# Gated cross-attention and mixture of experts: the last routing step's rows at the far end of each expert's slots, and sixteen products ahead of them

## The chip, the cores and the metric

The kernel runs on one core of a Trainium2 chip. The metric is the device time of one execution in microseconds (us); the median of the runs counts. A profiled execution gives the trace from which single instructions are read.

## The reference

The computation is one decoder block on 4096 tokens of width D = 512. First comes a layernorm, a gated attention to 3202 context rows and a residual. Then comes a layernorm, a router that gives each token its two best of eight experts, the experts (512 to 2048 to 512, exact gelu), and a gated residual. Cut to the second part:

```python
gates = softmax(xf @ w_router + b_router)
topv, topi = top_k(gates, 2)
cap = int(1.25 * n / e)                      # 640 slots for each expert
pos = cumsum(one_hot(topi.reshape(-1)), axis=0)[...] - 1
keep = pos < cap                             # later rows are dropped
buf[e_flat, min(pos, cap - 1)] += where(keep, xf[tok], 0)
h = gelu(buf @ w1 + b1)
out = h @ w2 + b2
y = sum over k of w[:, k] * out[e, pos]      # w: gate, 0 if not kept
y = y / max(sum of w, 1e-6)
x = x + tanh(g_ffn) * y
```

The order of the tokens decides only who is kept when an expert has more than 640. Which of its slots a kept row takes doesn't matter to the result, as long as the row is brought back to its own token.

## The kernel before

The work that concerns the change is the end of the routing pass and the beginning of the experts.

**Routing pass.** The 4096 tokens are 32 tiles of 128. `STEPS` groups them: six steps of four tiles and then four steps of two. For a tile, `tile_mm` (line 1045) does eight accumulating matmuls into a bank pair `x1p` (line 1062), 264 columns each, which give the attention's output and the router's logits together. DVE adds the residual (`x1`, line 1066), ACT squares it for the variance (`jx`, line 1072) and stores the row. When a step's tiles are done, `scale` (line 1086) computes `rstd` on GpSimd (POOL, lines 1090 and 1091). `choose` (line 1093) takes the logits to one-hot choices on DVE, ending in `mask` (line 1149) and the running counts `base` (line 1157), while ACT writes the normalized rows `xn`. `place` (line 1159) lets PE count positions (`pos`, a matmul with a triangle of ones, `upper`, on `mask`, and one with `ones` on `base`, lines 1167 and 1168), and DVE turns them into slot indices `sidx` and weights. `dispatch` (line 1193) sends one tile's rows for one choice to their slots in the DRAM buffer `buf_d`: an indirect DMA issued by POOL, called a scatter here (line 1198). There are 64 scatters, two for each tile.

A step is software-pipelined over the next: `choose` of a step is written ahead of the tiles of the next one, `place` after the first two tiles of it (in a step of four tiles in the middle of the step, in one of two at its end), and `send` writes the scatters in groups of four or five around `scale`. `issue_after` pins an instruction's place in its engine's order to another one. On POOL a scatter that is written ahead of `rstd` runs ahead of it.

After the last tile PE has no tile left while the last step is chosen, placed and sent. `idle_work` fills that with matmuls whose result is not used: 7 of them ahead of the last `pos` and 11 behind it (line 1218).

**Experts.** Each expert's 640 slots are five blocks of 128. `expert_in` (line 1328) loads a block from `buf_d` (`xb`, issued by SP), transposes it on PE (`bps`, line 110) and copies it to `bT` (line 1344). For expert 0 each load waits for all 64 scatters. A product of two 2-by-2 blocked matrices is done with seven block products instead of eight (`seven`, line 1295); its block sums are taken on DVE (`T1` to `T4` of the rows, `w1s` of the weights). A product is `prod`: two accumulating matmuls, 320 columns in the first layer. The first layer has four such groups f for each half of the 2048 columns. In a group the order is `pa` (A11 B11, copied to `p1` by ACT), `p6`, `p7`, `pb`, then A12 B21 added to `pa`, whose gelu ACT writes to `h`, `p4`, and the rest of `pb`. DVE adds the parts (`u2`, `u3`, `h`). The products are named `pah`, `p6h` and so on in the profile (line 1299). After four groups comes the matmul chain `op` (line 1462) and the second layer.

Of the kernel before, what the change touches and what calls it, by code (L numbers as in the profile page):

```python
# [6 lines left out]
F32 = mybir.dt.float32  # L7
I32 = mybir.dt.int32
AF = mybir.ActivationFunctionType
# [5 lines left out]
P = 128  # L15
# [5 lines left out]
def gated_layer(ctx, tc, x, x_t, ctxt, ctxt_t, ctxt_c, ctxt_r, g_xattn, g_ffn, w_sim, w_sim_r, b_sim, W_qv, W_qv_t, b_qv, b_qv_c, w_router, b_router, w1, b1, w2, b2, out):  # L21
# [84 lines left out]
    def transposed(pool, src, name):  # L106

        ps = pool.tile([P, DC, P], F32, name=name, tag="tr")
        for c in range(DC):
            nc.tensor.transpose(ps[:, c, :], src[:, c * P : (c + 1) * P], ident)  # L110
        return ps

# [862 lines left out]
    with ExitStack() as s2:  # L975
# [49 lines left out]
        scatters = []  # L1025


        STEPS = [list(range(t, t + G)) for t in range(0, NT - 2 * G, G)]
        STEPS += [list(range(t, t + G // 2)) for t in range(NT - 2 * G, NT, G // 2)]
        qTs = {}  # L1030
        tt, ts, red = nc.vector.tensor_tensor, nc.vector.tensor_scalar, nc.vector.tensor_reduce
        stt = nc.vector.scalar_tensor_tensor
# [15 lines left out]
        def tile_mm(s, i):  # L1048
            t = s.tiles[i]
            g, q = divmod(t, 4)  # L1050
            if g not in qTs:
                qTs[g] = sb.tile([P, DC, TG], F32, name=f"q2T{g}", tag="q2T")
                ld = nc.sync.dma_start(qTs[g], qT_d[g])
                if g == 3:
                    with tc.issue_after(ld.ins):
                        load_half(0, 0)
            r = sb.tile([P, 2, BW], F32, name=f"r2_{t}", tag="r2", bufs=6)
            nc.sync.dma_start(r, r_d[t])
            ps = ps_mm.tile([P, 2, 512], F32, name=f"x1p{t}", tag="mm")
            for j in range(2):  # L1060
                for c in range(DC):
                    mm = nc.tensor.matmul(  # L1062
                        ps[:, j, :B1], qTs[g][:, c, q * P : (q + 1) * P], W1[:, c, j, :], start=(c == 0), stop=(c == DC - 1)
                    )
            x1 = sb.tile([P, D], F32, name=f"x1_{t}", tag="x1", bufs=G + 2)
            stt(
                x1.rearrange("p (j d) -> p j d", j=2), ps[:, :, :256], tgx, r[:, :, :256], ALU.mult, ALU.add,
                accum_out=s.sum[:, i : i + 1],
            )
# [23 lines left out]
        def choose(s):  # L1093
# [56 lines left out]
            for i in range(n):  # L1150
                if i + 1 < n:
                    dst = s.base[:, i + 1, :]
                elif s.next is not None:
                    dst = s.next.base[:, 0, :]
                else:
                    continue
                tt(dst, s.base[:, i, :], s.mask[:, i, :], ALU.add)

        def place(s):

# [33 lines left out]
            if s.next is not None and s.next.n == 2:  # L1194
                placed.append(done.ins)

        def dispatch(s, i, k):
            sc = nc.gpsimd.indirect_dma_start(
                out=buf_d[:, :],
                out_offset=bass.IndirectOffsetOnAxis(ap=s.sidx[:, k, i : i + 1], axis=0),  # L1200
                in_=s.xn[:, i, :],
                in_offset=None,
                bounds_check=E * CAP - 1,
                oob_is_err=False,
            )
            scatters.append(sc.ins)

            tc.declare_no_dep(scatters[-1], group="scatters", reason="slots are unique")
            tc.add_to_no_dep_group("scatters", scatters[-1])

        placed = []
        def idle_work(mm, n):

            for _ in range(n):
                with tc.issue_after(mm.ins):
                    mm = nc.tensor.matmul(idle, ones, wv[:, 0, :], start=True, stop=True)
            return mm

        idle = ps_id.tile([P, D], F32, name="idle", tag="idle")
        prev, s = None, begin(0)
        nc.vector.tensor_copy(s.base[:, 0, :], first_i)
        routed = []

        def send(n):
            for _ in range(min(n, len(routed))):
                dispatch(*routed.pop(0))

        def place_prev():  # L1230
            if prev is not None:
# [2 lines left out]

        for g in range(len(STEPS)):
            s.next = begin(g + 1) if g + 1 < len(STEPS) else None
            if prev is not None:
                choose(prev)
            for i in range(2):
                mm = tile_mm(s, i)  # L1240
            if s.n > 2:
                with tc.issue_after(mm.ins):
                    place_prev()
                send(4)
                for i in range(2, s.n):
                    tile_mm(s, i)
            sc = scale(s)
            if s.n == 2:
                with tc.issue_after(mm.ins):
                    place_prev()  # L1250
            with tc.issue_after(sc.ins):
# [14 lines left out]
    with ExitStack() as s3:  # L1266
# [25 lines left out]
            tt(S4, A12, S2, ALU.subtract)  # L1292
            return tt(A21, A11, A21, ALU.subtract)

        def seven(tag, n, A11, A12, A22, S1, S2, S3, S4, B11, B21, B22, T1, T2, T3, T4, done):

            def prod(ps, A, B, start=True, stop=True):
                for i, (a, b) in enumerate(zip(A, B)):
                    nc.tensor.matmul(  # L1299
                        ps, a, b, start=start and i == 0, stop=stop and i == len(A) - 1, skip_group_check=True  # L1300
                    )

            pa = bank(f"pa{tag}")[:, :n]
            prod(pa, A11, B11, stop=False)
            p1 = sb.tile([P, HC], F32, name=f"p1{tag}", tag="p1")[:, :n]
            nc.scalar.copy(p1, pa)  # L1306
# [11 lines left out]
            prod(pa, A12, B21, start=False)  # L1318
            done("11", pa, None)
            p4 = bank(f"p4{tag}")[:, :n]  # L1320
            prod(p4, A22, T4)
            done("21", p4, u3)
# [2 lines left out]

        row_loads, summed = [], {}

        def expert_in(e):
# [3 lines left out]
            xbs = []  # L1332
            for s in range(NST):
                xb = sb.tile([P, R], F32, name=f"xb{e}_{s}", tag="xb", bufs=NST)
                ld = nc.sync.dma_start(xb, buf_d[e * CAP + s * P : e * CAP + (s + 1) * P, :])
                row_loads.append(ld.ins)
                if e == 0:
                    for i in scatters:
                        tc.add_manual_dep(
                            ld.ins, i.name, mybir.DependencyInfo(mybir.DependencyClass.Sync, mybir.DependencyReason.DATA),  # L1340
                            reason="every token is in its slot",
                        )
                ps = transposed(ps_tr, xb, f"bps{e}_{s}")
                (nc.vector.tensor_copy if s % 2 else nc.scalar.copy)(xT[:, :, s * P : (s + 1) * P], ps)
# [39 lines left out]

        stored = []
        w1s = w1_sums(0, 0)
        nxt = expert_in(0)
        with tc.issue_after(row_loads[-1]):
            load_half(0, 1)
        for e in range(E):  # L1390
# [16 lines left out]
            for h in range(2):  # L1407
                W2 = weights.pop((e, h))[1] if (e, h) != (0, 0) else weights[0, 0][1]
                weights[e, h] = (None, W2)
                hT = cb.tile([P, KH, CAP], F32, name=f"h{e}_{h}", tag="h")  # L1410
                hS = [cb.tile([P, KQ, MH], F32, name=f"hs{k}_{e}_{h}", tag=f"hs{k}") for k in (1, 2, 4)]
                for f in range(KQ):
                    col = e * NF + h * KH + f
# [16 lines left out]
                    seven(f"h{e}_{h}_{f}", HC, *A, *xs, hidden)  # L1430

                    left_sums(
                        hS[0][:, f, :], hS[1][:, f, :], hS[2][:, f, :],
# [120 lines left out]
```

## Time and profile before

| | |
|---|---|
| three runs | 2636.52, 2637.51 and 2645.64 us |
| median | 2637.51 us |
| profiled execution, its own time | 2642.18 us |
| its span in the trace | 2640.2 us |
| mean granted TensorE clock | 0.995 |
| PE busy | 2609.3 us, 99% |
| DVE, ACT, POOL busy | 1703.0, 462.6 and 236.6 us |
| routing matmuls `x1p` | 512 records, 117.5 us |
| expert transposes of block 0 start | 1631.75 us |
| `p6h` of the first group starts | 1639.34 us |
| `op` of the first half starts | 1667.43 us |

Times within the trace count from the start of the span. Each matmul of 32-bit floats shows as two records or so, so counts of records are larger than those in the code. PE, PEld, DVE, ACT, POOL and SP are the matmul and the weight load of TensorE, VectorE, ScalarE, GpSimd and the queue engine SyncE. A row of the profile gives the line, engine, operation, output and inputs, the number, the busy time and mean duration of one, and then the idle time of the engine ahead of it with what ended most of it.

### The profile page before, as it was taken

What the parts mean: (1) busy time and instruction counts of PE and PEld (TensorE: products, weight loads), DVE (VectorE), ACT (ScalarE), POOL (GpSimd) and SP (SyncE); (2) the same over time, 40 slices, a digit from 0 to 9 for tenths busy, and PEclk for the clock granted to TensorE, in tenths of its full rate; (3) what the DMA queues carried; (4) which work ended last, traced back from release to release, by engine and by line L of the source; (5) the groups of instructions that cost most, each with busy time, mean ns of one, the idle gap of its engine ahead of it and who ended that gap; (6) DMA issues with size and microseconds to landing.
All of it is one profiled execution on the core that took longest, in us unless ns stands there. A gap on an engine that the chain in (4) does not pass through costs nothing. (4 is left out here: it accounts for less than half of the span.)

```text
span 2640.2 us, 29718 instructions
## 1 busy us (share of the span) xinstructions
PE 2609.3 (99%) x11236; PEld 2104.7 (80%) x11236; DVE 1703.0 (65%) x3412; ACT 462.6 (18%) x796; POOL 236.6 (9%) x288
## 2 busy tenths in 40 slices
PE   8999999999999999999999998999999999999998
PEld 7748888888888888888888885777777777777776
DVE  7868856947768569478475566474757565565654
ACT  1201201201102002012020143212121111111111
POOL 0111000000001000000000155010101010101010
PEclk9999999999999999999999999999999999999999
DMA  8496656746747657467445794231324132223210
GB/s 316 150 290 234 207 180 192 244 149 179 255 158 196 220 162 239 159 189 245 153 144 203 279 351 162 79 124 64 128 72 145 71 128 88 104 92 100 76 60 20
DMA packets 182959, 436.07 MB, mean 165 GB/s; under 512 B 17454, under 2 KB 84270, under 8 KB 180768
## 3 DMA queue, kind: packets, MB, share of 16 engines
q1 hardware_dynamic: 150208, 352.25, 40.4%
q0 software_dynamic: 16096, 45.04, 5.0%
q10 hardware_dynamic: 16512, 36.88, 4.0%
q8 instruction: 89, 1.46, 0.2%
q14 instruction: 54, 0.44, 0.1%
HBM read 355.71 MB, written 85.55 MB: 167 GB/s over the span
## 5 line engine op out<-in xcount | busy, mean ns | idle before, releaser
L512 PE MATMUL pas<-Qp,kt 128*128 128x256 f32 x672 | 160.5, 380 | 0.0
L1299 PE MATMUL pah<-bT,w 128*128 128x320 f32 x512 | 159.3, 433 | 0.5 <-ACT p1h L1306 0.5
L662 PE MATMUL pbv<-E,vt 128*128 128x256 f32 x672 | 147.3, 379 | 0.0
L662 PEld LDWEIGHTS pbv<-E,vt 128*128 128x128 f32 x672 | 127.7, 190 | 17.4
L512 PEld LDWEIGHTS pas<-Qp,kt 128*128 128x128 f32 x672 | 127.1, 190 | 17.4 <-ACT hqT L720 0.2
L1299 PEld LDWEIGHTS pah<-bT,w 128*128 128x128 f32 x512 | 97.0, 190 | 39.7 <-ACT p1h L1306 1.0
L602 DVE TENSOR_TENSOR E<-E,mb 128x1024 f32<-128x1024 f32 x96 | 116.2, 1226 | 11.8 <-ACT mb L589 11.8
L603 ACT ACTIVATE E<-E 128x1024 f32<-128x1024 f32 x96 | 101.0, 1058 | 129.5 <-DVE E L602 128.7
L1299 PE MATMUL pao<-w,h 128*128 128x256 f32 x512 | 120.9, 379 | 0.0
L1062 PE MATMUL x1p<-W,q2T 128*128 128x264 f32 x512 | 117.5, 391 | 0.0
L1485 POOL DMA_INDIRECT out<-acc,ti x40 | 41.1, 1027 | 851.6 <-DVE acc L1484 841.8
L1462 PE MATMUL op<-w,h 128*128 128x512 f32 x256 | 114.8, 592 | 0.0
L1299 PEld LDWEIGHTS pao<-w,h 128*128 128x128 f32 x512 | 97.3, 190 | 20.1 <-issue 7.7
L1062 PEld LDWEIGHTS x1p<-W,q2T 128*128 128x128 f32 x512 | 97.8, 192 | 16.5
L468 ACT COPY p1s<-pas 128x512 f32<-128x512 f32 x48 | 28.1, 586 | 439.1 <-issue 257.0
L538 DVE TENSOR_TENSOR M<-M,E 128x1024 f32<-128x1024 f32 x80 | 98.0, 1225 | 4.3
L693 PE MATMUL vv<-E,vc 128*128 128x512 f32 x192 | 95.2, 627 | 0.0
L1462 PEld LDWEIGHTS op<-w,h 128*128 128x128 f32 x256 | 46.6, 190 | 48.7 <-issue 43.0
L1423 DVE TENSOR_TENSOR h<-p4h,u3h 128x320 f32<-128x320 f32 x64 | 31.3, 490 | 78.0 <-PE p4h L1299 76.3
L481 ACT COPY E<-pas 128x512 f32<-128x512 f32 x48 | 28.1, 586 | 303.9 <-PE pas L512 287.6
L484 DVE TENSOR_TENSOR E<-p4s,u3s 128x512 f32<-128x512 f32 x48 | 33.1, 689 | 73.5 <-PE p4s L512 73.5
L611 DVE TENSOR_TENSOR SM<-SM,E 128x1024 f32<-128x1024 f32 x64 | 78.7, 1229 | 2.5 <-ACT E L603 2.5
(449 smaller groups left out, 5470.4 us busy)
## 6 DMA issues: line engine op xcount, KB each, us to landing
kt<-kt_d SPq DMA_DIRECT2D x84, 896.0 KB
w<-in_w SPq DMA_DIRECT2D x32, 2048.0 KB
vt<-vs_d SPq DMA_DIRECT2D x56, 768.0 KB
wp<-wt_d SPq DMA_DIRECT2D x56, 520.0 KB
kt_d<-ktb ACTq DMA_DIRECT2D x12, 896.0 KB
buf_d<-zero SPq DMA_DIRECT2D x80, 129.0 KB
xb<-buf_d SPq DMA_DIRECT2D x40, 258.0 KB
r<-r_d SPq DMA_DIRECT2D x32, 260.0 KB
```

The lines of the kernel that those rows point to most:

```text
L484: tt(done(1, 0), p4, u3, ALU.add)
L512: nc.tensor.matmul(ps[:, jl, :], kts[j][:, KSLOT[p], k, :], B[p][:, k, :], start=start and jl == 0 and k == 0, stop=stop and k == 1, skip_ ...
L538: tt(M, M, e[:, :, h], ALU.max)
L602: live[g]["last"] = tt(e, e, m, ALU.subtract)
L603: live[g]["exp"] = nc.scalar.activation(e, e, AF.Exp)
L611: tt(SM, E_t[0][:, lr] if jj == 1 else SM, E_t[jj][:, lr], ALU.add)
L662: nc.tensor.matmul(ps[b], vt[:, j - i * JH, b * P : (b + 1) * P], right(j) if j < NJ else right_c, start=start and j == 0 and b == 0, stop ...
L693: mm = nc.tensor.matmul(ps[b], vc[:, h, b * P : (b + 1) * P], E[j // 2][:, :, h, j % 2, :] if j < NJ else ec, start=j == 0 and h == 0, sto ...
L1062: mm = nc.tensor.matmul(ps[:, j, :B1], qTs[g][:, c, q * P : (q + 1) * P], W1[:, c, j, :], start=(c == 0), stop=(c == DC - 1))
L1299: nc.tensor.matmul(ps, a, b, start=start and i == 0, stop=stop and i == len(A) - 1, skip_group_check=True)
L1462: nc.tensor.matmul(ps, hT[:, k, 2 * MH :], W2[:, k, :], start=(k == 0), stop=(k == KH - 1))
L1485: sc = nc.gpsimd.indirect_dma_start(out=out[:, :], out_offset=rows_of(ti, s), in_=acc[:, :], in_offset=None, bounds_check=N - 1, oob_is_er ...
```

## The change

1. The last twelve tiles are stepped 3, 3, 2, 2, 2 where they were 4, 2, 2, 2, 2: the sizes are five steps of four and then these five.
2. The last step's rows take the slots from the far end of each expert (the last slot first) instead of those behind the earlier rows. For this one matmul (`first`) sums the counts, and four DVE operations turn the position round. The last step's four scatters are kept in a list of their own, `late`. Of expert 0's five blocks the first three wait for the 60 other scatters alone, the last two for all.
3. For expert 0, `early_products` does A11 B11 and A12 B21 of the four groups of the first half (16 matmuls, `pe`) as soon as the first three blocks are transposed. `seven` then leaves these two products out in those groups. The order on PE is block 0, 1, 2, products of f = 0, 1 and 2, blocks 3 and 4, products of f = 3.
4. `idle_work` does 7 and 5 matmuls where it did 7 and 11, with the identity, broadcast, as moving operand in place of `wv`.
5. Places in the engines' orders: the second tile's `x1` in steps of two follows `choose`'s count, scatters are chained one after the other, the groups of `send` are 4, 3 or 5 by the size of the step. Block 1's copy to `bT` is ACT's for expert 0.

```diff
-        STEPS = [list(range(t, t + G)) for t in range(0, NT - 2 * G, G)]
-        STEPS += [list(range(t, t + G // 2)) for t in range(NT - 2 * G, NT, G // 2)]
+        STEPS, sizes = [], [G] * (NT // G - 3) + [3, 3, 2, 2, 2]
...
+            with tc.issue_after(chosen[-1]) if s.n == 2 and i else ExitStack():
+                stt(x1..., accum_out=s.sum[:, i : i + 1])
...
+            if s.next is None:
+                before = T("before", [P, 2, n, E])
+                tt(before, s.first.unsqueeze(1).unsqueeze(1).to_broadcast([P, 2, n, E]), s.oh, ALU.mult)
+                s.far = T("far", [P, 2, n])
+                red(s.far, before, AX.X, ALU.add)
+                stt(s.far, s.rv, -float(CAP), s.far, ALU.mult, ALU.add)
...
+            if s.next is None:
+                stt(pos, s.far, float((E + 1) * CAP - 1), pos, ALU.add, ALU.subtract)
...
-            scatters.append(sc.ins)
+            (scatters if s.next is not None else late).append(sc.ins)
...
-                    mm = nc.tensor.matmul(idle, ones, wv[:, 0, :], start=True, stop=True)
+                    mm = nc.tensor.matmul(idle, ones, ident.unsqueeze(1).to_broadcast([P, 4, P]), start=True, stop=True)
...
-                send(4)
+                with tc.issue_after(scaled[-1].ins) if scaled else ExitStack():
+                    send(4)
...
+                s.first = ps_mm.tile([P, 2, 512], F32, name="first", tag="mm")[:, 0, :E]
+                    mm = nc.tensor.matmul(s.first, ones, s.base[:, 0, :], start=True, stop=True)
...
-                send(4 if s.n > 2 else 5)
+                send({4: 4, 3: 3, 2: 5}[s.n])
...
-        idle_work(prev.counted, 11)
+        idle_work(prev.counted, 5)
...
-                    for i in scatters:
+                    for i in scatters if (s + 1) * P <= CAP - len(late) // 2 * P else scatters + late:
...
+                if amid is not None and s * P < HC <= (s + 1) * P:
+                    between = amid(*([xT[:, k, :HC] for k in c] for c in ((0, 1), (2, 3))))
+                    behind = [next(between) for _ in range(KQ - 1)][-1]
...
+        def early_products(B11, B21):
+            early["h"] = hT = cb.tile([P, KH, CAP], F32, name="h0_0", tag="h")
+            mm = None
+            for f in range(KQ):
+                A11, A12 = ([a[:, k, f * P : (f + 1) * P] for k in range(2)] for a in w1s[:2])
+                pa = bank(f"pe{f}")[:, :HC]
+                with tc.issue_after(mm.ins) if mm is not None else ExitStack():
+                    prod(pa, A11, B11, stop=False)
+                early[f] = cb.tile([P, D], F32, name=f"e1_{f}", tag=f"o{f}")[:, :HC]
+                nc.scalar.copy(early[f], pa)
+                last = prod(pa, A12, B21, start=False)
+                nc.scalar.activation(hT[:, f, :HC], pa, AF.Gelu, bias=b1_t[:, f : f + 1])
+                mm = yield last
```

More of the change, by code (lines that the diff above doesn't have):

```diff
@@ L109, in transposed @@
         for c in range(DC):
-            nc.tensor.transpose(ps[:, c, :], src[:, c * P : (c + 1) * P], ident)
+            moved.append(nc.tensor.transpose(ps[:, c, :], src[:, c * P : (c + 1) * P], ident))
         return ps
+    moved = []
     NJ = L // (2 * P)
@@ L1023, in gated_layer @@
         nc.gpsimd.iota(first_i, pattern=[[NST, E]], base=0, channel_multiplier=0)
-        scatters = []
-        STEPS = [list(range(t, t + G)) for t in range(0, NT - 2 * G, G)]
-        STEPS += [list(range(t, t + G // 2)) for t in range(NT - 2 * G, NT, G // 2)]
+        scatters, late = [], []
+        STEPS, sizes = [], [G] * (NT // G - 3) + [3, 3, 2, 2, 2]
+        for n in sizes:
+            t = STEPS[-1][-1] + 1 if STEPS else 0
+            STEPS.append(list(range(t, t + n)))
+        assert STEPS[-1][-1] == NT - 1
         qTs = {}
@@ L1065, in tile_mm @@
             x1 = sb.tile([P, D], F32, name=f"x1_{t}", tag="x1", bufs=G + 2)
[L1066 to L1069, printed above, removed]
+            with tc.issue_after(chosen[-1]) if s.n == 2 and i else ExitStack():
+                stt(
+                    x1.rearrange("p (j d) -> p j d", j=2), ps[:, :, :256], tgx, r[:, :, :256], ALU.mult, ALU.add,
+                    accum_out=s.sum[:, i : i + 1],
+                )
             junk = sb.tile([P, D], F32, name=f"jx{t}", tag="jx", bufs=2)
@@ L1156, in choose @@
                     continue
-                tt(dst, s.base[:, i, :], s.mask[:, i, :], ALU.add)
+                chosen.append(tt(dst, s.base[:, i, :], s.mask[:, i, :], ALU.add).ins)
+            if s.next is None:
[4 more added lines that the diff above has]
+                stt(s.far, s.rv, -float(CAP), s.far, ALU.mult, ALU.add)
         def place(s):
@@ L1193, in place @@
             )
-            if s.next is not None and s.next.n == 2:
+            if s.next is not None and s.next.n < G:
                 placed.append(done.ins)
@@ L1205, in dispatch @@
             )
-            scatters.append(sc.ins)
-            tc.declare_no_dep(scatters[-1], group="scatters", reason="slots are unique")
-            tc.add_to_no_dep_group("scatters", scatters[-1])
-        placed = []
+            (scatters if s.next is not None else late).append(sc.ins)
+            tc.declare_no_dep(sc.ins, group="scatters", reason="slots are unique")
+            tc.add_to_no_dep_group("scatters", sc.ins)
+        placed, chosen = [], []
         def idle_work(mm, n):
@@ L1217, in idle_work @@
                 with tc.issue_after(mm.ins):
-                    mm = nc.tensor.matmul(idle, ones, wv[:, 0, :], start=True, stop=True)
+                    mm = nc.tensor.matmul(idle, ones, ident.unsqueeze(1).to_broadcast([P, 4, P]), start=True, stop=True)
             return mm
         idle = ps_id.tile([P, D], F32, name="idle", tag="idle")
-        prev, s = None, begin(0)
+        prev, s, scaled = None, begin(0), []
         nc.vector.tensor_copy(s.base[:, 0, :], first_i)
@@ L1227, in send @@
             for _ in range(min(n, len(routed))):
-                dispatch(*routed.pop(0))
+                with tc.issue_after((scatters[-1:] + late[-1:])[-1]) if scatters else ExitStack():
+                    dispatch(*routed.pop(0))
         def place_prev():
@@ L1247, in gated_layer @@
             sc = scale(s)
+            scaled.append(sc)
             if s.n == 2:
@@ L1250, in gated_layer @@
                     place_prev()
+                mm = prev.counted
+            if s.next is None:
+                s.first = ps_mm.tile([P, 2, 512], F32, name="first", tag="mm")[:, 0, :E]
+                with tc.issue_after(mm.ins):
+                    mm = nc.tensor.matmul(s.first, ones, s.base[:, 0, :], start=True, stop=True)
             with tc.issue_after(sc.ins):
-                send(4 if s.n > 2 else 5)
+                send({4: 4, 3: 3, 2: 5}[s.n])
             prev, s = s, s.next
@@ L1293, in left_sums, with prod, seven @@
             return tt(A21, A11, A21, ALU.subtract)
[L1295 to L1306, printed above, removed]
+        def prod(ps, A, B, start=True, stop=True):
+            for i, (a, b) in enumerate(zip(A, B)):
+                mm = nc.tensor.matmul(
+                    ps, a, b, start=start and i == 0, stop=stop and i == len(A) - 1, skip_group_check=True
+                )
+            return mm
+        def seven(tag, n, A11, A12, A22, S1, S2, S3, S4, B11, B21, B22, T1, T2, T3, T4, done, p1=None):
+            there = p1 is not None
+            if not there:
+                pa = bank(f"pa{tag}")[:, :n]
+                prod(pa, A11, B11, stop=False)
+                p1 = sb.tile([P, HC], F32, name=f"p1{tag}", tag="p1")[:, :n]
+                nc.scalar.copy(p1, pa)
             p6 = bank(f"p6{tag}")[:, :n]
@@ L1317, in seven @@
             done("22", pb, u3)
-            prod(pa, A12, B21, start=False)
-            done("11", pa, None)
+            if not there:
+                prod(pa, A12, B21, start=False)
+                done("11", pa, None)
             p4 = bank(f"p4{tag}")[:, :n]
@@ L1326, in gated_layer, with expert_in @@
         row_loads, summed = [], {}
-        def expert_in(e):
+        def expert_in(e, amid=None):
             xT = cb.tile([P, DC, CAP], F32, name=f"bT{e}", tag="bT")
@@ L1331, in expert_in @@
             ti = sb.tile([P, NST], I32, name=f"ti{e}", tag="ti", bufs=E)
-            xbs = []
+            xbs, behind = [], None
             for s in range(NST):
@@ L1342, in expert_in @@
                         )
-                ps = transposed(ps_tr, xb, f"bps{e}_{s}")
-                (nc.vector.tensor_copy if s % 2 else nc.scalar.copy)(xT[:, :, s * P : (s + 1) * P], ps)
-                xbs.append(xb)
+                with tc.issue_after(behind.ins) if behind is not None else ExitStack():
+                    ps = transposed(ps_tr, xb, f"bps{e}_{s}")
+                (nc.vector.tensor_copy if s % 2 and (amid is None or s > 2) else nc.scalar.copy)(
+                    xT[:, :, s * P : (s + 1) * P], ps
+                )
+                xbs.append(xb)
+                if amid is not None and s * P < HC <= (s + 1) * P:
+                    between = amid(*([xT[:, k, :HC] for k in c] for c in ((0, 1), (2, 3))))
+                    behind = [next(between) for _ in range(KQ - 1)][-1]
+            if amid is not None:
+                between.send(moved[-1])
             B11, B12, B21, B22 = (xT[:, r : r + 2, c : c + HC] for r in (0, 2) for c in (0, HC))
@@ L1386, in gated_layer @@
         w1s = w1_sums(0, 0)
-        nxt = expert_in(0)
+        early = {}
+        def early_products(B11, B21):
[5 more added lines that the diff above has]
+                with tc.issue_after(mm.ins) if mm is not None else ExitStack():
+                    prod(pa, A11, B11, stop=False)
+                early[f] = cb.tile([P, D], F32, name=f"e1_{f}", tag=f"o{f}")[:, :HC]
[3 more added lines that the diff above has]
+                mm = yield last
+        nxt = expert_in(0, early_products)
         with tc.issue_after(row_loads[-1]):
@@ L1409, in gated_layer @@
                 weights[e, h] = (None, W2)
-                hT = cb.tile([P, KH, CAP], F32, name=f"h{e}_{h}", tag="h")
+                hT = early.pop("h") if "h" in early else cb.tile([P, KH, CAP], F32, name=f"h{e}_{h}", tag="h")
                 hS = [cb.tile([P, KQ, MH], F32, name=f"hs{k}_{e}_{h}", tag=f"hs{k}") for k in (1, 2, 4)]
@@ L1429, in gated_layer @@
                     A = [[a[:, k, f * P : (f + 1) * P] for k in range(2)] for a in w1s]
-                    seven(f"h{e}_{h}_{f}", HC, *A, *xs, hidden)
+                    seven(f"h{e}_{h}_{f}", HC, *A, *xs, hidden, early.pop(f, None))
                     left_sums(
```

## The prediction

> **What bounds the kernel now.** I read the page first, its busy shares and its costliest groups.
>
> ```profile
> PE 2609.3 (99%) x11236; PEld 2104.7 (80%) x11236; DVE 1703.0 (65%) x3412; ACT 462.6 (18%) x796; POOL 236.6 (9%) x288
> ...
> L1299 PE MATMUL pah<-bT,w 128*128 128x320 f32 x512 | 159.3, 433 | 0.5 <-ACT p1h L1306 0.5
> ...
> L1062 PE MATMUL x1p<-W,q2T 128*128 128x264 f32 x512 | 117.5, 391 | 0.0
> ```
>
> TensorE (PE) is busy 99% of 2640.2 us, so the whole change plays for the time in which PE has nothing useful, at the passage from the routing pass to the experts. That passage is seen in the table of windows (after the length, each engine's busy time, PE first; third from the right PE's clock) and then in the timeline of PE:
>
> ```profile
> 1598.00:1600.00 2.00, 0.28 (x2) 0.00 (x0) 1.83 (x13) 1.21 (x4) 1.39 (x3) 1.00 0.40 144
> 1600.00:1602.00 2.00, 1.43 (x6) 1.36 (x7) 0.69 (x5) 0.00 (x0) 0.88 (x1) 0.70 0.10 22
> 1602.00:1604.00 2.00, 2.00 (x6) 1.49 (x6) 1.81 (x9) 0.81 (x2) 0.20 (x1) 0.50 0.10 38
> ...
> 1632.00:1634.00 2.00, 2.00 (x10) 1.73 (x10) 0.27 (x1) 0.59 (x1) 0.00 (x0) 0.50 0.99 314
> ```
>
> ```profile
> 1600.57 0.37 PE L1167 MATMUL pos<-mask,upper 128*128 128x16 f32 x2 [2.29 <-DVE eq L1131]
> ...
> 1610.26 6.25 PE L1218 MATMUL idle<-wv,ones 128*128 128x512 f32 x14
> 1617.90 0.37 PE L1167 MATMUL pos<-mask,upper 128*128 128x16 f32 x2 [1.39 <-DVE mask L1149]
> 1618.12 0.37 PE L1168 MATMUL pos<-base,ones 128*128 128x16 f32 x2
> 1618.34 9.69 PE L1218 MATMUL idle<-wv,ones 128*128 128x512 f32 x22
> 1631.75 3.59 PE L110 MATMUL bps<-ident,xb 128*128 128x128 f32 x16 [3.72 <-DMA xb<-buf_d]
> ```
>
> The last tile of x1p ends at 1610.1; the first transpose of expert rows (bps) starts at 1631.75. Between them stand filler (idle, two records for each matmul of 0.86 to 0.88 us), pos, and 1.39 and 3.72 us of nothing. What ends last there is the chain of scatter, DMA and load, in the timeline of POOL:
>
> ```profile
> 1619.28 0.98 POOL L1198 DMA_INDIRECT buf_d<-xn,sidx  x1 [0.30 <-issue]
> 1621.54 1.23 POOL L1198 DMA_INDIRECT buf_d<-xn,sidx  x1 [1.28 <-issue]
> ...
> 1626.61 0.98 POOL L1198 DMA_INDIRECT buf_d<-xn,sidx  x1 [0.30 <-issue]
> ```
>
> The last scatter ends at 1627.59, SP issues the row loads at 1628.99, bps starts 2.76 later. PE then needs until 1639.34 for p6h of f=0, from where it has no gap.
>
> **What the Trainium skill says.** "TensorE: Matmul & The Clock Gate", Part 1, has the clock halved after an idle window of about 3.4 us that runs freely. The trace agrees in kind: after the 2.29 and the 3.72 us gaps PE ran 3.41 us at 0.50, costing 1.7 us each; after 1.39 it did not. "DMA: Bandwidth & Descriptors", on one DMA's anatomy, gives about 2.0 us fixed; the 2.76 us from load issue to transpose fits. "ScalarE: Activation LUTs", on ACT_TABLE_LOAD, gives 1283 ns; the trace has 1.28 at 1639.41, before the first gelu.
>
> **The change part by part**, on the clock of the profiled execution. That took 2642.18 (span 2640.2 plus 1.98), 4.67 above the median 2637.51. I put this down to its gap at 1598.28 to 1600.57: DVE's x of tile 28 waited 1.80 us for a signal that came 2.8 us after that tile's last matmul, then came the half clock: 2.3 + 1.7 of the 4.67. So an ordinary execution has p6h at about 1639.34 - 4.67 = 1634.7.
>
> 1. *Early products.* 16 matmuls are 8 products; one is 2 x 538 = 1.076 us (320 columns, pace of the h stage: 26 products in the 28.1 us to 1667.43). Before, 2 of them stand ahead of p6h, so 6 x 1.076 = 6.46 us move from behind it to ahead of it. It is a gain only if PE has free time there.
>
> 2. *Late step apart.* Blocks 0 to 2 need only the first 60 scatters; scatter 60 ended at 1620.26 where the last ended at 1627.59. So up to 7.3 us come free, if scatter 60 doesn't move. Blocks 3 and 4 still wait for all 64; SP holds xb3, xb4 and the loads of the next half's weights behind that wait, none of them needed earlier than 3 us after pe starts.
>
> 3. *Step sizes.* Sizes 4,4,2,2,2,2 at the end become 4,3,3,2,2,2 (tiles 20-22, 23-25). In a step of over two tiles, pos of the step before stands after two tiles of the next: pos(5) now stands behind tile 24, not 25. Its mask needs rstd(5), which on POOL stands behind four scatters of step 4. They ran at 1571.74 to 1576.54, started by xn(4), and the change doesn't touch that. So rstd(5) ends at 1577.8 (1.3 us for the pair), mask 3.8 later (choose with a stt inside took 3.74 to 3.88) at 1581.6. PE is through tile 24 at 1578.5: **3.3 us idle**. pos(5) 1581.85, tile 25 from 1582.6. Next, place(5) (2.4, and 0.75 to the first scatter) puts three scatters at 1586.45 to 1590.05 ahead of rstd(6): mask(6) 1595.1, pos(6) 1595.35; tile 27 ended at 1593.2: **2.15 us idle**. A half clock after the first gap (1.7) is hidden in the second. Then tiles 28 to 31 run to 1610.9, with no wait at pos(7) (its 2 tiles are 7.1, the chain 5.9) and 0.6 at pos(8). An ordinary run of before, without the lateness, has x1p end at 1606.1. So these stalls give back 4.8 us.
>
> 4. *The tail after.* pos(8) 1611.5, xn 1614.9, four scatters 1615.65 to 1620.8 (0.97 + 0.30 each), loads 1.4 later, bps at **1624.9**. Filler is 12 instead of 18, ending at about 1623.0 (6 x 0.87 = 5.2 less): 1.9 us idle, between a gap that halved the clock and one that did not. pe starts after three blocks, 3.5 later, 1628.4. Six products take 6.46; ACT has behind them the table load (1.28), four copies of 0.43 and gelus of 0.53 which must release banks: I take 1.65 us of waits. 1636.5 less the overlaps: 1636.1. bps 3 and 4, 1.8; the last two products and a copy, 2.8: p6h at **1640.8**. The late scatters end near 1628, so their blocks are there by 1632 and don't bind.
>
> 5. *Small parts.* first: one matmul of 128x8, under 0.3 us on PE, in filler's place. before, far and two stt: four DVE operations of about 0.2 us; one (0.2) lies on the late scatters' path, which has 4 us of slack; the others beside filler. Chained dispatches: POOL issues in that order already, nothing; if the cover of POOL's spare time were gone it would be 0.3 each. The broadcast identity instead of wv in filler: same columns, bound -0.1 to +0.1 each, hidden by the gap. b_1's load ahead on SP: 64 KB, 0.3 us, behind the row loads.
>
> The copy of block 1 on ACT instead of DVE takes 0.59 for 0.69: nothing, since blocks arrive about 1 us apart. The second tile's stt after choose in steps of two tiles: at most 0.75 earlier mask, 0.75 later rstd; choose without a stt inside took 2.98. I take zero and keep both ends.
>
> Sum: p6h at 1640.8 with 6.46 less behind it counts as 1634.3, against 1639.34 in the profiled execution (-5.0) and 1634.7 in an ordinary run (-0.4). With half a chance of 1.7 for the 1.9 us gap it is +0.5; if the ACT waits vanish (bound 0 to 1.65) it is -1.2. An ordinary run at 2637.5 - 1.2 to + 0.5; I take the lower half, **2636.5**.
>
> **The rivals.**
>
> *A, about the same (0.52): 2634.5 to 2638.5*, as summed.
>
> *B, the tail's gain stays (0.30): 2630 to 2634.* For it: PE's gaps at pos(5) and pos(6) rest on POOL's pace, and the second exists only if scatters of step 5 are ready before rstd(6)'s input; were rstd(6) first, 2.15 us are back, and with the ACT waits gone 3.8: 2637.1 - 3.8 = 2633.3; without the first gap too, 2630. Or the lateness of tile 28 is regular in before and goes with the new order: again 2.3 to 4. Against it: POOL's order in the change has rstd(5) behind four scatters, and two of three runs lie 5 us below the profiled one.
>
> *C, slower (0.15): 2639.5 to 2644.* In the first f groups PE has 5 products each instead of 7: 20 x 1.076 = 21.5 us. DVE was busy 22.24 of the 28.09 us of that stretch, and its work doesn't shrink. If DVE sets the pace, PE waits from f=1 on for banks: 22.24 - 21.5 = 0.7, with the T sums of 0.8 each that now lie nearer 2 to 3; a throttle at both gaps that isn't hidden adds up to 3.4: 2637.1 + 2 to 6. It decides when DVE is more than 90% busy between p6h and op. Against: w2 sums (4 x 1.22) can be done during op's 4.7 us.
>
> *D, the change doesn't do what it says (0.03):* the wait on SP or bank reuse keeps pe behind the late scatters; then 2637 to 2641.
>
> **How the numbers follow.** A measurement of this kernel can tell about 0.5%, 13.2 us, from no change. No part reaches it: all that could be gained is the 6.46 moved plus 5 of tail, all that was priced as a loss 5 + 3.4. So within 0.5% has 0.94, faster 0.04 (several unknowns at once), slower 0.02 (before's own runs reach 2645.64). The forecast is A's, 2636.5. The range takes B from 2630 and C up to 2642.
>
> **What would show it.** In the profile after: PE idle 3 us ahead of pos after tile 24 and 2 us ahead of the next pos, released by DVE mask; bps 5 to 7 us earlier (1624 to 1626); the gap ahead of it about 2 us; six pe products with short waits on ACT before bps 3; p6h near 1641; h stage without PE gaps. Wrong if PE has no gap at those pos (then B), if p6h to op takes over 23 us (C), or if bps 0 starts after the last scatter's landing (D).

## The result, and the profile after

The changed kernel takes 2645.4 us (median of 7 runs, 2645.22 to 2647.45), against 2637.51 before (7 runs): a ratio of 1.003, 95% interval 1.002 to 1.0039. It is 7.9 us slower. The forecast was 2636.5 with a range up to 2642.0. So a small gain was forecast and a loss measured; the time is still within 0.5% of before's, as the forecast also said.

The page of the changed kernel has PE busy for the same share as before. PE's work is shorter by 5 us, about what six filler matmuls took, in a longer span:

```profile
span 2643.3 us, 29700 instructions
...
PE 2604.4 (99%) x11226; PEld 2102.5 (80%) x11226; DVE 1700.6 (64%) x3415; ACT 462.8 (18%) x797; POOL 227.5 (9%) x288
```

The timeline of PE shows where the time is (start, length, then what; in brackets the idle time ahead and what ended it):

```profile
1582.58 0.59 PE L1181 MATMUL pos<-mask,upper 128*128 128x24 f32 x2 [3.12 <-DVE mask L1156]
1583.00 0.60 PE L1182 MATMUL pos<-base,ones 128*128 128x24 f32 x2
1583.43 13.68 PE L1068 MATMUL x1p<-W,q2T 128*128 128x264 f32 x48
...
1619.98 4.54 PE L1235 MATMUL idle<-ident,ones 128*128 128x512 f32 x10
1633.67 3.02 PE L110 MATMUL bps<-ident,xb 128*128 128x128 f32 x12 [9.16 <-DMA xb<-buf_d]
1637.37 4.82 PE L1324 MATMUL pe<-bT,w 128*128 128x320 f32 x16 [0.68 <-ACT bT L1378]
1642.84 2.42 PE L1324 MATMUL pe<-bT,w 128*128 128x320 f32 x8 [0.65 <-ACT e L1440]
...
1648.90 1.24 PE L1324 MATMUL p6h<-x,w1s 128*128 128x320 f32 x4
```

The gap at pos(5) is there, 3.12 us long. But the first bps stands at 1633.67, where 1624.9 was forecast, behind a gap of 9.16 us. POOL and SP say why:

```profile
1620.92 0.98 POOL L1214 DMA_INDIRECT buf_d<-xn,sidx  x1 [0.30 <-issue]
1623.28 1.23 POOL L1214 DMA_INDIRECT buf_d<-xn,sidx  x1 [1.38 <-issue]
...
1628.36 0.98 POOL L1214 DMA_INDIRECT buf_d<-xn,sidx  x1 [0.30 <-issue]
```

```profile
1630.74 2.23 SPq L1367 DMA_DIRECT2D xb<-buf_d  x5
```

The first row is scatter 60, issued by 1621.90. The load of block 0 is not issued behind it but at 1630.74, 1.4 us after the end of scatter 64. All five loads go out together within 2.23 us, as they did before. So the last step's rows are not apart from the others: the loads still wait for them.

For comparing traces I count from pos of step 4. Up to about there all versions do the same work in the same order, and what they do differently comes behind it. Executions reach it at 1564.9 to 1568.9, and that of free at 1574.2, where PE stood still for 4.53 us ahead of pos(2) and had a half clock behind it. "Rest" runs from p6h to the end of the trace. The row of before is an execution of 2638.38 us, near its median; the trace shown ahead of the prediction is of a slower one. Its bps and p6h are these:

```profile
1628.34 3.71 PE L110 MATMUL bps<-ident,xb 128*128 128x128 f32 x16 [3.78 <-DMA xb<-buf_d]
...
1635.53 1.34 PE L1299 MATMUL p6h<-x,w1s 128*128 128x320 f32 x4
```

| us from pos(4) | last x1p ends | scatter 60 ends | scatter 64 ends | first load | first bps | p6h | rest |
|---|---|---|---|---|---|---|---|
| before (2638.38) | 39.67 | 50.52 | 57.64 | 59.04 | 61.87 | 69.06 | 1000.82 |
| after (2645.33) | 44.96 | 54.22 | 61.65 | 63.05 | 65.99 | 81.22 | 994.41 |
| free | 43.79 | 53.05 | 60.72 | 54.47 | 57.33 | 71.82 | 994.41 |
| oldsteps | 39.66 | 48.83 | 55.84 | 57.24 | 60.08 | 76.70 | 994.41 |
| free_oldsteps | 39.66 | 48.83 | 55.84 | 50.24 | 53.13 | 69.94 | 994.41 |
| steps_only | 49.11 | 57.94 | 65.20 | 66.60 | 69.42 | 77.10 | 1000.82 |
| late_alone | 39.68 | 48.86 | 55.89 | 50.27 | 53.28 | 65.78 | 1000.71 |
| fill7 | 39.65 | 48.81 | 55.82 | 50.22 | 53.23 | 67.49 | 994.41 |
| fill7_gelu | 39.65 | 48.84 | 55.84 | 50.24 | 53.13 | 67.51 | 994.41 |
| rstd_first | 42.76 | 51.61 | 59.00 | 53.02 | 55.83 | 73.32 | 994.41 |
| idle11 | 43.78 | 56.28 | 63.61 | 65.02 | 67.79 | 84.42 | 994.40 |

The first two rows account for the whole difference between these two executions: p6h comes 12.16 later, the rest is 6.41 shorter, the start 1.21 later. That is 6.96 in sum, and their times differ by 6.95.

### The profile page after: what moved, and what is told of

Read it like the earlier page. It is cut to its first block, busy times and chain, and to the rows that moved or that the text cites. A ratio compares the mean times of both kernels' runs of the same rounds, so it can differ in the third digit from the quotient of the medians.

```text
span 2643.3 us, 29700 instructions
## 1 busy us (share of the span) xinstructions
PE 2604.4 (99%) x11226; PEld 2102.5 (80%) x11226; DVE 1700.6 (64%) x3415; ACT 462.8 (18%) x797; POOL 227.5 (9%) x288
## 5 line engine op out<-in xcount | busy, mean ns | idle before, releaser
L1324 PE MATMUL pah<-bT,w 128*128 128x320 f32 x480 | 148.8, 432 | 0.0
L1324 PEld LDWEIGHTS pah<-bT,w 128*128 128x128 f32 x480 | 91.2, 190 | 36.4
L1324 PE MATMUL p7h<-bT,w 128*128 128x320 f32 x256 | 79.5, 432 | 0.0
L514 PE MATMUL pbs<-Qp,kt 128*128 128x256 f32 x336 | 79.5, 379 | 0.0
```

Of the source, the lines that this page charges most:

```text
L514: nc.tensor.matmul(ps[:, jl, :], kts[j][:, KSLOT[p], k, :], B[p][:, k, :], start=start and jl == 0 and k == 0, stop=stop and k == 1, skip_ ...
L1324: mm = nc.tensor.matmul(ps, a, b, start=start and i == 0, stop=stop and i == len(A) - 1, skip_group_check=True)
```

## The experiments

All change the changed kernel unless it is said otherwise. Ratios are to before's runs on the same chip (95% intervals); medians of different chips are less comparable. None of the versions is as much as 0.5% away from before, so the differences are told from one another by these intervals and by the traces.

**free: the wait taken away.** What made the first load wait was not the list of 60 that the change writes, but a dependency that the programming layer adds by itself: a load from `buf_d` waits for the buffer's last writer, and that is scatter 64. One statement declares the two independent:

```diff
+                    if (s + 1) * P <= CAP - len(late) // 2 * P:
+                        for i in late:
+                            tc.declare_no_dep(ld.ins, i, reason="the late rows take other slots")
```

In the built program one number changes in the first load's waits. It waits for one semaphore on each of eight scatter lanes; on lane 6, which carries scatter 64, it waited for 224 and now for 208, one scatter fewer. The load of block 3 gets the 224.

> The changed kernel with one statement more: the loads of blocks 0 to 2 of expert 0 are declared free of the four late scatters. Theory W (a wait that the change meant to remove is still there: the buffer of rows is followed as one tensor, so block 0's load waits for its last writer, the late scatter 64): scatter 60 was issued by 1621.9 and landed by 1623.2, so the load moves from 1630.8 to about 1623.4, the first bps from 1633.67 to about 1626.1, and with it the end by 7.6, up to 8.8 if the half clock at the first bps goes too: 2636.6 to 2637.8. Theory S (all of the loss is PE's stalls in the last routing steps): 2645.4, unchanged. Theory C (VectorE is the bound in the first layer): the first bps is earlier, but the end gains less than half, above 2641.

Measured: 2635.53 (13 runs), ratio 0.9988 (0.998 to 0.9997), from 1.003. The loads now split, in the timeline of SP and of PE:

```profile
1628.67 8.38 SPq L1367 DMA_DIRECT2D xb<-buf_d  x5
```

```profile
1631.53 0.63 PE L110 MATMUL bps<-ident,xb 128*128 128x128 f32 x4 [1.64 <-DMA xb<-buf_d]
```

The five loads take 8.38 us to go out instead of 2.23, as only the last two still wait for the late scatters. The first is issued 1.42 us behind the end of scatter 60 (table: 54.47 and 53.05), where it was 8.83 in the changed kernel. The gap ahead of the first bps falls from 9.16 to 1.64. Theory W holds; S and C fall. Of the 9.40 us by which p6h comes earlier in the table, 7.49 are this wait (from scatter 60 to the first bps, 4.28 for 11.77). The other 1.9 are half clocks that the trace of after has, at pos(5) and at bps, and that of free has not.

**oldsteps: the step sizes undone.**

```diff
-[G] * (NT // G - 3) + [3, 3, 2, 2, 2]
+[G] * (NT // G - 2) + [2, 2, 2, 2]
```

> The changed kernel with the step sizes of before (six of 4, four of 2), the wait on the last scatter kept. Theory W with the stalls of the prediction (4.8; the trace after has x1p end 1612.65 where 1606.1 was worked out for before, of which 0.7 was there before the stretch began): 2645.4 - 4.8 to - 6.0 = 2639.4 to 2640.6, no gap of over 1 us ahead of pos, the gap ahead of bps still 8 to 9 us. If the sizes don't matter: 2645.4. If they are the whole loss: 2637.5.

Measured: 2640.44 (13 runs), ratio 1.0006 (0.9998 to 1.0014). The last x1p ends 5.3 us earlier than after's, and the gap ahead of the first bps is 9.01. So sizes and wait are two separate losses; the sizes cost 5.0 us by the medians and 6.3 by the ratios. With the wait alone the change is about even with before: while the first load waits for scatter 64, the early products change their place without filling idle time.

**free_oldsteps: both.** The two diffs above.

> Both edits: loads of blocks 0 to 2 free of the late scatters, step sizes of before. Theory W with stalls: both gains add up, 2645.4 - 7.6 - 5.4 = 2632.4, down to 2630.6 with the half clock gone: faster than before's 2637.5 by 5 to 7. If the two hide one another (a filler or the scatters' pace on POOL then bounds): 2636 to 2638.

Measured: 2633.76 (9 runs), ratio 0.9977 (0.9967 to 0.9987), 4.4 below before's 2638.12 on the same chip. The gains add up in the place of the first bps (53.13, 12.9 earlier than after) but not wholly in p6h: behind the 2.06 us gap ahead of bps PE's clock is halved. The table of windows shows the gap and the first 3.4 us behind it (third column from the right: the clock), and the timeline of PE the products that follow, still slow:

```profile
1620.00:1622.00 2.00, 0.00 (x1) 0.03 (x1) 2.00 (x3) 0.00 (x0) 1.51 (x2) 1.00 0.92 272
1622.00:1625.40 3.40, 2.80 (x12) 1.81 (x12) 0.57 (x1) 1.53 (x3) 3.10 (x4) 0.59 0.29 92
```

```profile
1625.68 6.41 PE L1324 MATMUL pe<-bT,w 128*128 128x320 f32 x16 [0.67 <-ACT bT L1380]
```

**steps_only: the sizes alone, in the kernel before.**

```diff
-        STEPS = [list(range(t, t + G)) for t in range(0, NT - 2 * G, G)]
-        STEPS += [list(range(t, t + G // 2)) for t in range(NT - 2 * G, NT, G // 2)]
+        STEPS = []
+        for n in [G] * (NT // G - 3) + [3, 3, 2, 2, 2]:
+            t = STEPS[-1][-1] + 1 if STEPS else 0
+            STEPS.append(list(range(t, t + n)))
...
-                send(4 if s.n > 2 else 5)
+                send({4: 4, 3: 3, 2: 5}[s.n])
```

> The kernel before with only the step sizes of the change (3, 3, 2, 2, 2 at the end, scatters grouped 4, 3, 5). Theory S part: PE idle 3 us ahead of pos after tile 24 with a half clock behind it; 2637.5 + 4.8 to + 6.0 = 2642.3 to 2643.5. If the sizes don't matter: 2637.5. If they are worth a gain by themselves (the last pos then comes earlier): below 2636.

Measured: 2647.17 (7 runs), ratio 1.0029 (1.0017 to 1.004): slower than forecast, 7.6 us by the ratio instead of 4.8 to 6.0. The gaps are longer than in the changed kernel, 4.33 and 2.82:

```profile
1583.27 0.59 PE L1169 MATMUL pos<-mask,upper 128*128 128x24 f32 x2 [4.33 <-DVE mask L1151]
...
1599.08 0.37 PE L1169 MATMUL pos<-mask,upper 128*128 128x24 f32 x2 [2.82 <-DVE mask L1151]
```

So one of the change's other edits to the order wins back part of what the sizes lose. In this trace POOL issues a scatter between the two instructions of rstd of step 5 (at 1577.25, between 1576.79 and 1578.28), and this rstd ends 12.03 us after pos(4); in the changed kernel no scatter stands there and it ends 10.80 after. The built programs show which edit does that: the chain of scatters, or the place of `send` behind the rstd of the step before. With either of the two alone the changed kernel is built to the same program, and the place of x1 behind the count changes nothing in it. At the old sizes none of the three does: on all engines before and oldsteps are the same program up to the end of the last x1p.

**rstd_first: free, with the scatters behind rstd in the steps of three.**

```diff
-                    send(4)
+                    send(4 if s.n == G else 0)
...
-                send({4: 4, 3: 3, 2: 5}[s.n])
+                send({4: 4, 3: 7, 2: 5}[s.n])
```

> The kernel free (2635.5, step sizes 4, 3, 3, 2, 2, 2) with the scatters of the steps of three all sent behind rstd instead of four ahead of it. Theory P (rstd stands on POOL behind four scatters, which is what PE waits for at pos): the gaps of 3.1 and 1.9 us ahead of these pos go, x1p ends 5 us earlier, 2630.5 to 2632. If the gaps come from VectorE's or ACT's own work: they stay, 2635.5. If the later scatters then hold up the end: gaps gone but 2635 or more.

Measured: 2633.98 (21 runs), ratio 0.9988 (0.9981 to 0.9994), no different from free's. Theory P is right on the cause: both gaps are gone. But the seven scatters now stand ahead of the next rstd. The timeline of POOL shows first how in the changed kernel rstd of step 5 follows the fourth scatter at once, and then how in rstd_first rstd of step 7 follows the seventh:

```profile
1576.28 0.98 POOL L1214 DMA_INDIRECT buf_d<-xn,sidx  x1 [0.30 <-issue]
1577.33 0.19 POOL L1097 TENSOR_SCALAR rstd<-ssd 128x3 f32<-128x3 f32 x1
```

```profile
1592.84 0.98 POOL L1214 DMA_INDIRECT buf_d<-xn,sidx  x1 [0.30 <-issue]
1593.89 0.19 POOL L1097 TENSOR_SCALAR rstd<-ssd 128x2 f32<-128x2 f32 x1
```

So most of the gain isn't had: a gap of 1.85 us appears one pos later, with a half clock (tiles 30 and 31 take 9.05 for 7.37):

```profile
1577.47 0.37 PE L1181 MATMUL pos<-mask,upper 128*128 128x24 f32 x2
...
1589.06 0.37 PE L1181 MATMUL pos<-mask,upper 128*128 128x24 f32 x2
...
1598.90 0.37 PE L1181 MATMUL pos<-mask,upper 128*128 128x16 f32 x2 [1.85 <-DVE mask L1156]
1599.12 0.38 PE L1182 MATMUL pos<-base,ones 128*128 128x16 f32 x2
1599.34 9.05 PE L1068 MATMUL x1p<-W,q2T 128*128 128x264 f32 x32
```

The first bps is 1.50 us earlier than in free, but a second half clock falls on the products behind it (16 records of pe take 7.33 for 4.82), and p6h is 1.50 later.

**late_alone: free_oldsteps without the early products.**

```diff
-        nxt = expert_in(0, early_products)
+        nxt = expert_in(0)
```

> The kernel free_oldsteps (2633.8) without the early products: the first three loads are still free of the late scatters, but PE does no products ahead of blocks 3 and 4. If the early products are what turns the early loads into time: bps of block 3 waits for the late scatters, loads at about 1626.6, p6h at about 1633.5 where free_oldsteps counts as 1632.3 (1638.8 less 6.46), so 2635.0, about 1.2 slower than free_oldsteps. If the early loads alone bring the gain: 2633.8 or below. If they bring nothing without the products: 2637 to 2638.5.

Measured: 2637.05 (13 runs), ratio 0.9999 (0.9991 to 1.0008). By the runs the early loads bring nothing by themselves: PE waits 4.13 us for block 3 instead.

```profile
1619.68 2.69 PE L110 MATMUL bps<-ident,xb 128*128 128x128 f32 x12 [2.16 <-DMA xb<-buf_d]
1626.51 1.94 PE L110 MATMUL bps<-ident,xb 128*128 128x128 f32 x8 [4.13 <-DMA xb<-buf_d]
```

Its profiled execution, at 2634.92, is among its fastest, so the table's row shows it better than the ratio does. The medians put the early products at 3.3 us once the loads are early, and the table at 2.1 (65.78 + 1000.71 against 69.94 + 994.41). The size is rough, but the intervals of late_alone and free_oldsteps (0.9967 to 0.9987) are apart.

**fill7 and fill7_gelu.** Two filler matmuls more in free_oldsteps, and then a small gelu ahead of the row copies.

```diff
-        idle_work(prev.counted, 5)
+        idle_work(prev.counted, 7)
...
+        g0 = sb.tile([P, 4], F32, name="g0", tag="g0", bufs=1)
+        nc.scalar.activation(g0, b1_t[:, :4], AF.Gelu)
```

> The kernel free_oldsteps (2633.8) with 7 instead of 5 filler matmuls behind the last pos. Theory H (the gap of 2.06 us ahead of the first bps halves PE's clock for 3.4 us, which costs about 1.6): the gap falls to 0.3, the clock stays, 2632.2. If the half clock there costs nothing, since blocks arrive slowly: 2633.8.

> The kernel fill7 with one gelu of 128x4 on ACT ahead of the row copies, so that the table load (1.28 us) is done before the first early product. Its first gelu and the copies of e behind it then come 1.28 earlier: the wait of 0.65 among the pe products goes, 0.6 to 1.3 faster than fill7: about 2631.3. If PE's waits there come from the copies alone: same as fill7.

Measured: 2631.24 (12 runs), ratio 0.9976 (0.9968 to 0.9985), and 2630.96 (13 runs), 0.9978 (0.9969 to 0.9986). In fill7's trace the gap ahead of bps is 0.45, the clock behind it is full, and 16 records of pe take 4.82 us for 6.41:

```profile
1619.81 2.06 PE L110 MATMUL bps<-ident,xb 128*128 128x128 f32 x12 [0.45 <-DMA xb<-buf_d]
```

```profile
1619.80:1623.20 3.40, 2.54 (x15) 1.74 (x16) 0.48 (x1) 1.76 (x3) 3.10 (x4) 1.00 0.27 88
```

From bps to p6h it takes 14.26 where free_oldsteps took 16.81. By medians that is 2.5 faster, but the ratios are almost the same (0.9976 and 0.9977), so the gain is seen in the trace and not settled by the runs. The gelu was a miss: the wait of 0.65 among the pe products goes, and one of 0.52 for the copy of e comes in its place a product later; from bps to p6h 14.38. fill7, fill7_gelu and free_oldsteps all beat both kernels, by 0.22 to 0.24% against before, and nothing here sets one of them above the others.

**idle11: the old filler in the changed kernel.**

```diff
-        idle_work(prev.counted, 5)
+        idle_work(prev.counted, 11)
```

> The changed kernel with 11 filler matmuls behind the last pos, as before, instead of 5; the wait on the last scatter kept. The gap of 9.2 us ahead of the first bps falls to about 4. If only the time of the first bps counts: 2645.4, unchanged, the half clock behind it as well[...]. If the shorter gap saves the half clock: 2643.8.

Measured: 2647.92 (9 runs), ratio 1.0026 (1.0016 to 1.0036), after's within the interval. The gap is 2.15 us and still halves the clock. In this trace the last scatter ends 2 us later than in after's, as VectorE waited 2.59 us ahead of the last tile's x1. By the ratios, the filler that the change took out is no part of the loss.

**before_again, before_third, before_fourth: before's own trace.**

> The kernel before, once more, for a second trace. The prediction took its 1600.57 gap, with 2.3 us of idle PE and a half clock behind it, for an accident of the first trace, and an ordinary execution for one with x1p ending at about 1606.1 and p6h at about 1634.7. If that is so: no gap over 1 us ahead of pos behind tile 29, and p6h within 1.5 of 1634.7 (the start of the stretch may differ by about 1). If the gap is regular: 2 us again, p6h at 1638 to 1640.

> The kernel before a third time: both traces so far are of executions of about 2642, 4 to 5 above the median of its other runs. From pos of step 4 to p6h they take 72.3 and 71.4 us; with everything else alike a run of 2637.8 would need 68.0. If this execution is near 2637 to 2638: the stretch takes about 68 and has no gap over 1 us ahead of a pos but the last. If it is near 2642 again: gaps of 1.4 to 2.3 there again, and what an execution at the median looks like stays open.

> The same once more, for the same reason: near 2637 to 2638 a stretch of about 68 us without a gap over 1 us ahead of pos but the last; near 2642 gaps of 1.4 to 2.3.

Measured: 2642.68, 2640.68 and 2638.38. From pos(4) to p6h they take 71.38, 70.12 and 69.06, and the trace of 2642.18 takes 72.35. The gaps ahead of pos are 1.53 and 1.43 in the first, 0.52, 0.76 and 0.88 in the second, 0.56 and 1.52 in the third. In each of the four traces VectorE stands still once or twice in the last routing steps, for 1.2 to 3.0 us in sum, for a signal whose sender the profile doesn't name ("remote"). In the trace of 2642.18 the longest is this, on tile 28:

```profile
1597.57 0.75 DVE L1066 SCALAR_TENSOR_TENSOR x<-x1p,gx,r 128x512 f32<-128x512 f32 x1 [1.80 <-remote]
```

The five versions with the old sizes (oldsteps, free_oldsteps, late_alone, fill7 and fill7_gelu) run the same program as before up to the last x1p. None of their traces has such a wait, and from pos(4) on no gap ahead of a pos is over 0.56. So the prediction's reading that the gap of 2.29 was an accident holds in this: the program doesn't make it. What makes it is open. The traces of these five are from one chip (11), the three later traces of before from two others (7 and 6), and idle11, the one changed version with such a wait, is from chip 7; no experiment separates the chips.

This bears on the table. The row of before holds 1.95 us of this wait, and scatter 60 ends 1.7 later there than in oldsteps. As an estimate, an execution of before without it has its first bps at 60.1, as oldsteps has, and p6h 7.2 to 8.7 later, as the four traces have: 67.3 to 68.8. The prediction had 67.7 (1634.7 less 1566.98). Against that the first bps of the changed kernel comes 5.9 us later, not 4.1.

## Why the prediction was wrong

**The step that failed is part 2**: "Blocks 0 to 2 need only the first 60 scatters". It was read from the list in the diff, and the "up to 7.3 us" that should "come free" rested on it. The kernel's loads have further waits that no line of it writes, and one of them was on the scatter that the change meant to leave behind. The first bps was forecast at 1624.9, which is 57.9 after pos(4) at 1566.98; free has 57.33, after has 65.99. Of this miss of 8.1 us, 7.4 is the time from scatter 60 to scatter 64. The error of the forecast is 8.9.

**Rival D** named this ("the wait on SP or bank reuse keeps pe behind the late scatters") and had 0.03 for a chance, which was far too little for something that the built program states outright. Its price was wrong too. By the prediction's own sum a bps 8.1 later gives 2636.5 + 8.1 = 2644.6; it said 2637 to 2641.

**Part 3 was right on the gaps.** The rstd behind four scatters, the gap at pos(5) of 3.3 (3.12 measured), the second at pos(6) of 2.15 (none in after, where a half clock filled it; 1.92 in free, where none came). The half clock was mis-sized: it was put at 1.7 us and wholly hidden in the second gap, but in after it lasts twice as long as in the trace of before (6.8 us, from 1582.2 to 1589.0, for 3.4) and is hidden only in part: the last x1p ends at 44.96 and in free at 43.79, apart by 1.17. The give-back was put at 4.8; it is 5.3 in after and 4.1 in free. With the gap at pos(5) there, the first ground of rival B was not met.

**Part 1 was right in size:** the rest behind p6h is 6.41 us shorter (994.41 for 1000.82), forecast 6.46. It counts only if PE has the time: with the wait kept (oldsteps) the change comes out even, with the wait gone (free_oldsteps) it gains.

**Part 4 was near where the wait is gone:** 1.4 us from scatter 60 to the load (1.42 in free). From bps to p6h it took 15.9, which is 1.4 too much (14.49 in free; 15.23 in after with its half clock). The ACT waits of 1.65 are 0.68, 0.65 and 0.52, 1.85 in all.

**Rival C fell.** VectorE is busy 20.42 of 21.50 us from p6h on, 95%, over the 90% that I gave as the point of decision. PE has no gap:

```profile
1648.90:1670.40 21.50, 21.50 (x80) 14.76 (x79) 20.42 (x58) 4.62 (x7) 6.24 (x5) 1.00 0.34 111
```

**Part 5 was right on x1**, which it took as zero and which changes nothing in the built program. Its "nothing" for the chained dispatches holds for the old sizes alone. With the new ones the chain, or the place of `send`, keeps a scatter out of rstd, 1.2 us at pos(5). The sum had rstd without that scatter, so this is no part of the error.

With the wait gone the forecast is near: free measures 2635.53 where 2636.5 was forecast. Against before on its chip that is 2.6 less by the medians, where 1.0 less was forecast; the 1.4 us of part 4 are most of the difference.

## What to carry to other kernels

When a change shortens a list of waits, don't cost it by the list: read every wait of the first instruction that is to start earlier, with its count, since a dependency that is added for the whole buffer can keep the very wait that was dropped. An earlier transfer and the work for the gap that it opens may be worth something only together: here 0.23% (free_oldsteps), where either of them alone brings nothing (late_alone has a ratio of 0.9999, oldsteps of 1.0006). And look where a stall goes when the order on one queue is turned: moving four scatters behind rstd cleared two gaps and made a third.

## What the runs showed of the hardware

The same gap doesn't always halve PE's clock. Ahead of pos(5) PE was idle 3.12 us in after and in free. After ran at half clock behind it until 1589.0 (in the second window below, 0.64 over 3.6 us is 2.6 us at 0.5 and the rest at 1); free ran at full clock:

```profile
1583.00:1586.40 3.40, 3.40 (x10) 2.78 (x11) 2.84 (x16) 1.01 (x3) 0.60 (x1) 0.50 0.84 254
1586.40:1590.00 3.60, 3.60 (x12) 2.85 (x11) 0.00 (x0) 0.00 (x0) 2.38 (x3) 0.64 0.33 121
```

```profile
1589.60:1593.00 3.40, 3.40 (x17) 2.95 (x18) 2.77 (x15) 1.01 (x3) 0.54 (x1) 1.00 0.90 256
```

The shortest single gap that was followed by a half clock is 1.69 us (free_oldsteps, ahead of pos(2) at 1536.17); one of 1.92 (free) was not. The clearest case is a gap of 2.28 or 2.29 us that all fourteen traces have at about 1457 us, ahead of a group of attention matmuls, `pad`. In eleven traces a half clock follows it, in fill7_gelu, rstd_first and idle11 none: the same 16 records of `pad` take 6.74 us in after and 3.74 in fill7_gelu. That agrees with what the Trainium skill says in "TensorE: Matmul & The Clock Gate", Part 1, that the window runs freely. The same part puts the half clock after an idle window of about 3.4 us; here gaps of 1.69 to 2.29 us were enough and one of 3.12 was not, so on the length of the gap the measurement decides. A gap ahead of critical work is therefore worth filling even where it is well under 3.4 us, as fill7's trace shows with one of 2.06.
